# Attention with routed experts on one core: block-wide additions in the last stage, shared-expert work moved ahead of the router's column transposition, and the first query tile projected earlier

## The chip, the cores and the metric

The kernel runs on one NeuronCore of a Trainium2 chip. The time is the device time of a whole run in microseconds (us). Three runs of the kernel before gave 494.02, 495.47 and 496.73 us; the median is 495.47 us.

A core has five engines, each with an instruction stream of its own: TensorE (PE, matrix products into PSUM; PEld is its weight load), VectorE (DVE), ScalarE (ACT), GpSimd (POOL) and SyncE (SP, here used to issue DMAs). DMAs can be issued from SP, ACT or POOL; each engine works through its stream in order, so a DMA that waits for its data holds up what stands behind it on the issuing engine.

## What is computed

All arithmetic is in float32; x has 32 sequences of 100 tokens with 256 features (3,200 tokens), the context 32 sequences of 361 rows with 192 features.

```python
x = x + cross_attention(layernorm(x), ctx)      # one head, E = 256, its own layer norms inside
n = layernorm(x)
shared = gelu(n @ ws1 + bs1) @ ws2 + bs2
aff    = softmax(n @ Wr + br)                   # 31 experts
routed = sum over the 3 best experts e of aff[e] * (gelu(n @ We1[e] + Be1[e]) @ We2[e] + Be2[e])
out    = x + (shared + routed + n)
```

## The kernel before, in words

Tokens lie in 25 tiles of 128, and four tiles make a block (`BLOCKS`: blocks 0 to 5 have four tiles, block 6 has one). `xb[k]` holds block k of the residual stream in SBUF as [128, tiles, 256]. The order on all engines is written out by hand (`manual_schedule`), so program order is execution order on each engine.

**Start.** Wq, Wk, Wv are transposed on TensorE (`transposed`, L300 to L311) and folded into one matrix for the scores (`fold_scores`). Statistics of context rows and tokens are taken on DVE, a rough inverse root on POOL (`rough`, L213, a power), and a Newton step on DVE (`newton`).

**Attention loop, i = 0 to 36** (`for i in range(B + 5)`, B = 32). Every iteration works on several stages at once: the context of sequence i is transposed (`ctx_transpose`, L484), the context of i + 1 normalised (`ctx_normalise`, L474 on ACT and L227 on DVE), the scores of i - 1 taken (`scores`, L492, which needs the projected queries `qk` of its tokens), their exponentials transposed (`exp_transpose`) and applied (`weighted`). `token_project(t)` (L452 on TensorE, L456 on ACT) writes the queries of tile t; for i = 0 that is tile 0, at the end of the iteration's main part. At the end of iteration 0 `transposed(wv_sb, ...)` transposes Wv, and in iteration 1 `bias_cols` (L318) makes Wv's bias columns.

**Router, in the same loop.** Each finished tile passes through `project_out`, `route_norm`, `route_turn` (tile `pl`, L631), `route_logits` (`pr`, L638), `route_choice` (DVE and ACT: the three best experts and a mask `mk`), `route_count` (`pp`, L677 to L681: how many tokens chose each expert so far; POOL adds the running sum, L684), `route_slots` and `route_scatter` (POOL, three indirect DMAs per tile, L559, that write the token's row into its experts' lists in DRAM). Tile 24 is the last: its logits come in iteration 35 (B + 3), its count in 36.

**Shared expert.** `shared_half(k, f, psum)` (L729) is half of a block's first layer, two products of 512 columns; `shared_gelu(k)` (L737) the activation of both halves; `shared_mm(t)` (L752, L755) a tile's second layer together with the gated output biases; `shared_add(t)` (L760) adds it to `xb`. In the loop block 0's halves stand at i = 33 (B + 1) and 35 (B + 3). After the loop come gelu of block 0 and both halves of block 1.

**From counts to experts** (L896 to L990). On DVE: counts are turned into tiles per expert and running ends (a doubling scan, L909, five additions of 31 elements over padded rows `run0`, `run1`), then into a start row and an expert for each of up to 105 expert tiles, two columns `both`. TensorE transposes these columns (`p_ec`, L938); from the result come the numbers with which SP addresses the expert weights and token rows (`fetch`), and the packed expert numbers that TensorE reads as registers. `shared_mm(0)` and `(1)` stand after that transposition, `(2)` ahead of the transposition `p_oh` (L975), `(3)` after it. Then the expert biases are gathered (L984), registers loaded, and block 1's shared second layer is done (`shared_second(1)`).

**Expert stage** (`run`, L1051 to L1084): 92 tiles, each turned, multiplied by its expert's two matrices, scaled and scattered to `y_d` by POOL. A rarely needed rest stands behind an If.

**Last stage** (`TAIL`). Letters and block numbers are the order: f = both halves and gelu of a block, e = its second layer with `shared_add`, t = `total_of`, s = `store`. For each tile `collect` loads the three expert outputs of 128 tokens (384 KB) through SP into one of 15 buffers. `total_of` adds y0 + y1 on POOL (L1147) and x + y2 and x + (y0 + y1) on DVE (L1148, L1149), 256 elements wide, tile by tile. `store` writes a block from ACT's queue (L1154):

```python
TAIL = "f2 f3 e2 t0 t1 f4 s0 s1 e3 t2 t3 f5 s2 s3 e4 t4 f6 s4 e5 t5 s5 e6 t6 s6"
```

Of the kernel before, what the change touches and what calls it, by code (L numbers as in the profile page):

```python
# [8 lines left out]
F32 = mybir.dt.float32  # L9
# [26 lines left out]
def xattn_ffn(  # L36
# [6 lines left out]
    P = 128  # L43
# [43 lines left out]
    def ps_t(name):  # L87
        return ps.tile([P, 512], F32, tag="tp", name=name)
# [303 lines left out]
    pool.memset(ones, 1.0)  # L392

    GM = 4
    PAD = 16
# [7 lines left out]
    for t in XG[0]:  # L403
# [5 lines left out]
    token_rstd(0)  # L409

    kk = iota_t([P, GM, KTOP], "kk", [[0, GM], [1, KTOP]])
    one, oh, onesf, *runs = (
        const.tile([P, n], F32, tag=name, name=name)
        for name, n in (("one", NE), ("oh", NG), ("onesf", P), ("run0", PAD + NE), ("run1", PAD + NE))
    )
    for t_ in (one, onesf):
        pool.memset(t_, 1.0)
    for t_ in (oh, b2z, *runs):
        pool.memset(t_, 0.0)

    mv2 = const.tile([P, NT, 2], F32, tag="mv2", name="mv2")
# [25 lines left out]
    def token_project(t):  # L447
        z = zT.pop(t)
        pq = ps_m(f"pq_{t}")
        for c, s, m in AUG:  # L450
            for d in range(2):
                nc.tensor.matmul(  # L452
                    pq[:m, c * P : (c + 1) * P], m_sb[:, d, s : s + m], z[:, d, :], start=(d == 0), stop=(d == 1)
                )
        for c, s, m in AUG:
            nc.scalar.activation(  # L456
                qk[:m, c, t * P : (t + 1) * P], pq[:m, c * P : (c + 1) * P], AF.Identity,
                bias=c_sb[:m, c : c + 1], scale=vcol[:m, c, G2 : G2 + 1],
            )
# [264 lines left out]
    def shared_half(k, f, psum):  # L724

        n = len(BLOCKS[k]) * P
        ph = phs[k, f] = psum(f"phs_{k}_{f}")
        for c in range(2):
            nc.tensor.matmul(  # L729
                ph[:, :n], ws1_sb[:, c, f::2], xT[k][:, c, :], start=(c == 0), stop=(c == 1)  # L730
            )
# [16 lines left out]
    def shared_mm(t):  # L748
        k, j = divmod(t, TPB)
        h, py = hs[k], ps_t(f"pys_{t}")  # L750
        for f in range(2):
            nc.tensor.matmul(  # L752
                py[:, :D1], h[:, f, j * P : (j + 1) * P], ws2_sb[:, f, :], start=(f == 0), stop=False
            )
        nc.tensor.matmul(py[:, :D1], gT[k], b2z[:, j, :], start=False, stop=True)  # L755
        pys[t] = py

    def shared_add(t):
        xt, _, _ = tile_of(t)
# [14 lines left out]
    def projected(i):  # L774

        return [t for t in range(NT) if t * P // L1 == i]
# [27 lines left out]
    for i in range(B + 5):  # L804
# [35 lines left out]
                route_transpose(t)  # L840
        if i < B:
            ctx_transpose(i)
        if i in crstd:
            ctx_rstd(crstd[i])
        if i + 1 < B:
# [14 lines left out]
            token_norm(t)  # L860
        for t in logits:
            route_logits(t)
        for t in projected(i):
            token_project(t)
        for t in projected(i + 1):
            token_transpose(t)
# [5 lines left out]
            project_out(t)  # L872
        if now:
            route_var(now)
        if i == 0:
            transposed(wv_sb, KD2, wvT, "v")
        if i == 1:
            bias_cols(wv_sb, KD2, B2, BV, lambda ec: wvT[:, ec, D2:DA], "bvc")
        if i == 2:
            fold_values()  # L880
# [2 lines left out]

        if i == B + 1:
            shared_half(0, 0, ps_t)
        if i == B + 3:
            shared_half(0, 1, ps_t)
    residual_factors(slice(EARLY * TPB, NT))
    shared_gelu(0)
    shared_first(1)  # L890

    att_ctx.close()

# [3 lines left out]
    def sel_t(shape, name, dt=F32):  # L897
        return sel.tile(shape, dt, tag=name, name=name)
# [4 lines left out]
    nc.vector.tensor_scalar(nt_i, cnt_i, 7, None, ALU.logical_shift_right)  # L903
    ntf = sel_t([P, NE], "ntf")
    nc.vector.tensor_copy(ntf, nt_i)
    nc.vector.tensor_copy(runs[0][:, PAD:], nt_i)
    cur, step = 0, 1
    while step < NE:
        nc.vector.tensor_tensor(  # L909
            runs[1 - cur][:, PAD:], runs[cur][:, PAD:], runs[cur][:, PAD - step : PAD - step + NE], ALU.add  # L910
        )
        cur, step = 1 - cur, 2 * step
    ends = runs[cur][:, PAD:]
    ind = sel_t([P, NE], "ind")
    ei = sel_t([P, 1], "ei")
    st0 = sel_t([P, 1], "st0")
# [3 lines left out]
    nc.vector.scalar_tensor_tensor(ind, iota0, ei, cnt, ALU.is_equal, ALU.mult, accum_out=nn)  # L920

    j128 = sel_t([P, 1], "j128")
    nc.vector.tensor_tensor(j128, iota_p, st0, ALU.subtract)
    nc.vector.tensor_scalar(j128, j128, float(P), None, ALU.mult)
    start = sel_t([P, 1], "start")
    nc.vector.scalar_tensor_tensor(start, nn, float(-P), j128, ALU.add, ALU.min)
    nc.vector.tensor_scalar(start, start, 0.0, None, ALU.max)
# [20 lines left out]
        nc.vector.scalar_tensor_tensor(ep, e4[:, :, k], float(1 << (BITS * k)), ep, ALU.mult, ALU.add)  # L948
    epT = sel_t([1, P // PACK], "epT", I32)
    nc.vector.tensor_copy(epT, ep)  # L950

    shared_mm(0)
    shared_mm(1)


    diag = sel_t([P, 2 * P], "diag")
# [13 lines left out]


    nc.vector.tensor_scalar(oh[:, :NE], iota0, ec, None, ALU.is_equal)
    shared_mm(2)
    pt = ps_t("p_oh")
    nc.tensor.transpose(pt[:NG, :P], oh, ident)  # L975
    ohT = sel_t([NG, P], "ohT")
    nc.scalar.copy(ohT, pt[:NG, :P])
    for t in range(2):
        shared_add(t)
    shared_mm(3)  # L980
    b1t = const.tile([P, 2, P], F32, tag="b1t", name="b1t")
    for c in range(2):
        pm = ps_m(f"p_b1_{c}")
# [149 lines left out]

    yv = y_d[: KTOP * T, :].rearrange("(t p k) d -> t p (k d)", p=P, k=KTOP)
    slot_ctx.close()
    ypool = ctx.enter_context(tc.tile_pool(name="ypool", bufs=15, reuse_waits="tile"))
    y3s = {}

    def collect(t):
        y3 = y3s[t] = ypool.tile([P, KTOP, D1], F32, tag="y3", name=f"y3_{t}")  # L1140
        reads("y", nc.sync.dma_start(y3.rearrange("p k d -> p (k d)"), yv[t]))

    def total_of(k):
        tiles = BLOCKS[k]
        for j, t in enumerate(tiles):
            y3, xt = y3s.pop(t), xb[k][:, j, :]
            nc.gpsimd.tensor_tensor(y3[:, 0, :], y3[:, 0, :], y3[:, 1, :], ALU.add)  # L1147
            nc.vector.tensor_tensor(xt, xt, y3[:, 2, :], ALU.add)  # L1148
            nc.vector.tensor_tensor(xt, xt, y3[:, 0, :], ALU.add)  # L1149
# [9 lines left out]
    for k in range(3):  # L1159
        for t in BLOCKS[k]:  # L1160
            collect(t)
    TAIL = "f2 f3 e2 t0 t1 f4 s0 s1 e3 t2 t3 f5 s2 s3 e4 t4 f6 s4 e5 t5 s5 e6 t6 s6"
    what = {"f": shared_first, "e": shared_second, "t": total_of, "s": store}
    with tc.manual_schedule(engines={ET.PE, ET.DVE, ET.Activation, ET.Pool}):
        for step in TAIL.split():
            k = int(step[1:])
            what[step[0]](k)
            if step[0] == "t" and k + 3 < len(BLOCKS):
                for t in BLOCKS[k + 3]:
                    collect(t)  # L1170


# [33 lines left out]
```

## Time and profile before

| quantity | value |
|---|---|
| median of three runs | 495.47 us |
| the profiled execution's own time | 495.27 us |
| span of its instructions | 493.5 us |
| mean granted TensorE clock | 0.971 |
| busy: PE, DVE, ACT, POOL | 458.0, 312.3, 248.8, 271.4 us |
| expert stage, about 250 to 440 us | 190 us, PE busy 189.09 |
| last stage, from the first `phs` at 441.56 us | DVE's last addition ends at 490.04 us |
| HBM | 68.27 MB read, 29.74 MB written |

The profile comes from one execution. A row of the timeline gives the start and the length in us, the engine, the line, the operation with its output and inputs, how many instructions were merged, and in brackets how long the engine had stood idle and what released it. Rows of the stretches give the busy time of each engine with its instruction count, then the granted clock of TensorE (1.00 is full speed), the share of time in which the DMA engines were busy and the GB/s they moved. The chain that ended last follows the work back from the last instruction to what released each step.

### The profile page before, as it was taken

How to read it: one execution, taken by the hardware profiler on the slowest of the kernel's cores; microseconds unless marked ns; L12 is line 12 of the kernel's file. 1: busy time of each engine (PE TensorE's matmuls, PEld its weight loads, DVE VectorE, ACT ScalarE, POOL GpSimd, SP SyncE). 2: the span in 40 equal slices, each digit the busy share in tenths (PEclk: the TensorE clock that was granted, in tenths of full speed). 3: DMA queues.
4: the chain of work that ended last, by engine and by line, in shares of the span. 5: the costliest groups of instructions: out<-in, count | busy, mean ns of one | idle time of the engine just before them, and what ended most of it. 6: DMA issues, size and time to landing. Idle time of an engine off the chain costs nothing. (4 is left out here: it accounts for less than half of the span.)

```text
span 493.5 us, 11028 instructions
## 1 busy us (share of the span) xinstructions
PE 458.0 (93%) x2976; PEld 399.5 (81%) x2976; DVE 312.3 (63%) x1280; ACT 248.8 (50%) x814; POOL 271.4 (55%) x544
## 2 busy tenths in 40 slices
PE   8799998998989999997899999999999999989964
PEld 8687877877878888874599999999999999966653
DVE  2789987988998877676554444444444434312995
ACT  2576776776878787745224444444444444432100
POOL 6322686885767575658305555555555555553750
PEclk9799998998999999998999999999999999999977
DMA  6889954453536811212578988888888889426992
GB/s 192 244 223 242 283 144 127 145 164 101 176 99 181 293 58 53 74 42 87 174 237 260 258 261 258 263 260 253 265 271 255 260 270 267 124 79 242 405 322 96
DMA packets 67783, 98.79 MB, mean 200 GB/s; under 512 B 8289, under 2 KB 43176, under 8 KB 67720
## 3 DMA queue, kind: packets, MB, share of 16 engines
q1 hardware_dynamic: 56360, 72.60, 50.8%
q0 software_dynamic: 8048, 22.17, 11.8%
q10 hardware_dynamic: 3312, 3.28, 1.9%
q8 instruction: 28, 0.46, 0.4%
q14 instruction: 35, 0.29, 0.2%
HBM read 68.27 MB, written 29.74 MB: 199 GB/s over the span
## 5 line engine op out<-in xcount | busy, mean ns | idle before, releaser
L559 POOL DMA_INDIRECT y_d<-ys,yrow x92 | 88.3, 960 | 100.3 <-ACT ys L1082 43.4
L1066 ACT ACTIVATE hT<-ph,b1t 128x128 f32<-128x128 f32 x184 | 57.5, 363 | 103.4 <-PE ph L1061 103.4
L1061 PE MATMUL ph<-xgT,w 128*128 128x128 f32 x736 | 101.8, 281 | 0.1
L1061 PEld LDWEIGHTS ph<-xgT,w 128*128 128x128 f32 x736 | 94.8, 197 | 0.4 <-DVE xgT L1053 0.3
L1076 PE MATMUL py<-w2r,hT 128*128 x368 | 94.3, 380 | 0.0
L559 POOL DMA_INDIRECT xs_d<-xl,su x75 | 75.1, 1001 | 28.2 <-issue 8.6
L1076 PEld LDWEIGHTS py<-w2r,hT 128*128 128x128 f32 x368 | 62.9, 190 | 4.8
L1084 DVE TENSOR_SCALAR ys<-py,gate 128x256 f32<-128x256 f32 x46 | 22.2, 484 | 65.4 <-PE py L1076 65.4
L1053 DVE COPY xgT<-pg 128x256 f32<-128x256 f32 x92 | 38.5, 420 | 33.8 <-PE pg L1051 33.8
L492 PE MATMUL pss<-z2T,qk 65*100 65x361 f32 (+1 forms) x128 | 45.7, 479 | 2.4 <-ACT qk L456 2.1
L521 PE MATMUL pcx<-exT,z 128*65 128x100 f32 (+3 forms) x384 | 45.5, 270 | 0.1
L521 PEld LDWEIGHTS pcx<-exT,z 128*65 128x65 f32 (+3 forms) x384 | 41.9, 172 | 0.6 <-ACT exT L508 0.6
L1051 PEld LDWEIGHTS pg<-ident,xg 128*128 128x128 f32 x184 | 35.6, 196 | 4.0
L1051 PE MATMUL pg<-ident,xg 128*128 128x128 f32 x184 | 35.5, 277 | 0.0
L752 PE MATMUL pys<-ws_sb,hs 128*128 128x256 f32 x100 | 27.7, 402 | 5.7 <-DVE x L760 4.6
L242 DVE BATCH_NORM_STATS2 stc<-z 128x6 f32<-128x192 f32 (+1 forms) x96 | 27.8, 344 | 6.9 <-DMA z<-in_ctx_dram 6.9
L1147 POOL TENSOR_TENSOR y<-y 128x256 f32<-128x256 f32 x25 | 20.2, 810 | 18.4 <-PE pys L755 9.2
L537 PE MATMUL po<-wvo,cT 128*128 128x257 f32 (+1 forms) x100 | 26.9, 391 | 3.0 <-ACT cT L528 2.8
L499 ACT ACTIVATE ex<-pss,nm 100x361 f32<-100x361 f32 x32 | 18.0, 562 | 22.3 <-DVE nm L497 19.0
L492 PEld LDWEIGHTS pss<-z2T,qk 65*100 65x100 f32 (+1 forms) x128 | 19.0, 168 | 12.6 <-ACT qk L456 3.5
L752 PEld LDWEIGHTS pys<-ws_sb,hs 128*128 128x128 f32 x100 | 19.8, 202 | 10.7 <-issue 7.8
L452 PE MATMUL pq<-zT,m_sb 128*128 128x128 f32 (+1 forms) x200 | 28.2, 284 | 0.0
(231 smaller groups left out, 868.5 us busy)
## 6 DMA issues: line engine op xcount, KB each, us to landing
w<-in_L_ffn_We_dram SPq DMA_DIRECT2D x92, 256.0 KB
xg<-xs_d SPq DMA_DIRECT2D x92, 131.5 KB
y<-y_d SPq DMA_DIRECT2D x25, 384.0 KB
w2r<-in_L_ffn_We_dram SPq DMA_DIRECT2D x31, 256.0 KB
z<-in_ctx_dram SPq DMA_DIRECT2D x32, 192.0 KB
xs_d<-none SPq DMA_DIRECT2D x3, 1052.0 KB
out_dram<-x ACTq DMA_DIRECT2D x6, 512.0 KB
x<-in_x_dram SPq DMA_DIRECT2D x5, 512.0 KB
```

The costliest lines, as they stand in the source:

```text
L242: nc.vector.bn_stats(st[:n, c, :], ztile[b][:n, c, :D2])
L452: nc.tensor.matmul(pq[:m, c * P : (c + 1) * P], m_sb[:, d, s : s + m], z[:, d, :], start=(d == 0), stop=(d == 1))
L492: nc.tensor.matmul(pss[:L1, :L2], qk[:m, a, b * L1 : (b + 1) * L1], z2T[:m, a, :], start=(a == 0), stop=(a == 1),)
L521: nc.tensor.matmul(pw[:m, :L1], z[:n, c, s : s + m], exT[:n, c, :], start=(c == 0), stop=(c == NCH - 1))
L537: nc.tensor.matmul(po[:, : D1 + 1], cT[:m, a, t * P % RING : t * P % RING + P], wvo[:m, a, :], start=(a == 0), stop=(a == 1))
L559: ins = nc.gpsimd.indirect_dma_start(out=dst, out_offset=bass.IndirectOffsetOnAxis(ap=index, axis=0), in_=src, in_offset=None).ins
L752: nc.tensor.matmul(py[:, :D1], h[:, f, j * P : (j + 1) * P], ws2_sb[:, f, :], start=(f == 0), stop=False)
L1051: nc.tensor.transpose(pt[:, c * P : (c + 1) * P], g[:, c::2], ident)
L1053: nc.vector.tensor_copy(xgT[i].rearrange("p c s -> p (c s)"), pt[:, : 2 * P])
L1061: nc.tensor.matmul(ph[:, f * P : (f + 1) * P], w1s[:, c, f::2], z[:, c, :], start=(c == 0), stop=(c == 1))
L1066: nc.scalar.activation(hT[i][:, f, :], ph[:, f * P : (f + 1) * P], AF.Gelu, bias=b1t[:, f, i : i + 1])
L1076: nc.tensor.matmul(py[:, :D1], h[:, f, :], w2f[:, bass.ds(e * (2 * D1) + f * D1, D1)], start=(f == 0), stop=(f == 1),)
```

## The change

- Last stage: `collect` loads a whole block into one buffer of [128, 4, 3, 256], still with one DMA a tile; five such buffers take the place of 15 tile buffers. `total_of` does all three additions on DVE, for blocks 0 to 4 over the whole block (1,024 elements a partition), for block 5 in two pairs of tiles (512), for block 6 over its one tile. The shared second layer is done in pairs: two tiles' products go into the two halves of one PSUM bank (`two_second`), and one addition of 512 takes them. Stores of blocks 0 to 4 are issued from POOL, those of 5 and 6 from ACT. The order in `TAIL` is new.
- Router's end: half (0, 1) moves from i = B + 3 to i = B + 2, half (1, 0) takes its place, and half (1, 1), tiles 0 and 1 of block 0 and block 1's gelu follow directly behind the loop, ahead of `p_ec`. Tiles 2 and 3 stand between `p_ec` and `p_bc`. `pys_3` takes its bank from the other PSUM ring.
- On DVE the doubling scan becomes one scan instruction, and j128 one instruction instead of two; the padded rows and their two memsets go.
- Start: tile 0 is projected in the middle of iteration 0, behind the transposition of context 0 and ahead of the normalisation of context 1; the transposition of Wv moves from iteration 0 to iteration 1.

```diff
@@ attention loop @@
         if i < B:
             ctx_transpose(i)
+        if i == 0:
+            for t in projected(i):
+                token_project(t)
...
-        for t in projected(i):
+        for t in projected(i) if i else ():
             token_project(t)
...
-        if i == 0:
+        if i == 1:
             transposed(wv_sb, KD2, wvT, "v")
-        if i == 1:
             bias_cols(wv_sb, KD2, B2, BV, lambda ec: wvT[:, ec, D2:DA], "bvc")
...
         if i == B + 1:
             shared_half(0, 0, ps_t)
+        if i == B + 2:
+            shared_half(0, 1, ps_t)
         if i == B + 3:
-            shared_half(0, 1, ps_t)
+            shared_half(1, 0, ps_m)
     residual_factors(slice(EARLY * TPB, NT))
     shared_gelu(0)
-    shared_first(1)
+    shared_half(1, 1, ps_m)
+    for t in range(2):
+        shared_mm(t)
+    shared_gelu(1)
@@ from counts to experts @@
-    nc.vector.tensor_copy(runs[0][:, PAD:], nt_i)
-    cur, step = 0, 1
-    while step < NE:
-        nc.vector.tensor_tensor(
-            runs[1 - cur][:, PAD:], runs[cur][:, PAD:], runs[cur][:, PAD - step : PAD - step + NE], ALU.add
-        )
-        cur, step = 1 - cur, 2 * step
-    ends = runs[cur][:, PAD:]
+    ends = sel_t([P, NE], "ends")
+    nc.vector.tensor_tensor_scan(ends, one, ntf, 0.0, ALU.mult, ALU.add)
...
-    nc.vector.tensor_tensor(j128, iota_p, st0, ALU.subtract)
-    nc.vector.tensor_scalar(j128, j128, float(P), None, ALU.mult)
+    nc.vector.tensor_scalar(j128, iota_p, st0, float(P), ALU.subtract, ALU.mult)
...
-    shared_mm(0)
-    shared_mm(1)
+    shared_mm(2)
+    pys[3] = ps_m("pys_3")
+    shared_mm(3, pys[3])
...
-    shared_mm(2)
     pt = ps_t("p_oh")
...
-    shared_mm(3)
@@ last stage @@
-    ypool = ctx.enter_context(tc.tile_pool(name="ypool", bufs=15, reuse_waits="tile"))
+    ypool = ctx.enter_context(tc.tile_pool(name="ypool", bufs=5, reuse_waits="tile"))
...
+    def collect(k):
+        y3 = y3s[k] = ypool.tile([P, TPB, KTOP, D1], F32, tag="y3", name=f"y3_{k}")
+        for j, t in enumerate(BLOCKS[k]):
+            reads("y", nc.sync.dma_start(y3[:, j, :, :].rearrange("p k d -> p (k d)"), yv[t]))
 
     def total_of(k):
-        tiles = BLOCKS[k]
-        for j, t in enumerate(tiles):
-            y3, xt = y3s.pop(t), xb[k][:, j, :]
-            nc.gpsimd.tensor_tensor(y3[:, 0, :], y3[:, 0, :], y3[:, 1, :], ALU.add)
-            nc.vector.tensor_tensor(xt, xt, y3[:, 2, :], ALU.add)
-            nc.vector.tensor_tensor(xt, xt, y3[:, 0, :], ALU.add)
+        y3 = y3s.pop(k)
+        n, width = len(BLOCKS[k]), TPB if k < len(BLOCKS) - 2 else TPB // 2
+        for j in range(0, n, width):
+            js = slice(j, min(j + width, n))
+            xt = xb[k][:, js, :]
+            nc.vector.tensor_tensor(y3[:, js, 0, :], y3[:, js, 0, :], y3[:, js, 1, :], ALU.add)
+            nc.vector.tensor_tensor(xt, xt, y3[:, js, 2, :], ALU.add)
+            nc.vector.tensor_tensor(xt, xt, y3[:, js, 0, :], ALU.add)
+
+    def two_second(k):
+        tiles = BLOCKS[k]
+        for j in range(0, len(tiles), 2):
+            pair = tiles[j : j + 2]
+            py = ps_t(f"pyt_{pair[0]}")
+            for i, t in enumerate(pair):
+                shared_mm(t, py[:, i * D1 : (i + 1) * D1])
+            xt = xb[k][:, j : j + len(pair), :].rearrange("p t d -> p (t d)")
+            nc.vector.tensor_tensor(xt, py[:, : len(pair) * D1], xt, ALU.add)
...
-        nc.scalar.dma_start(
+        eng = pool if k < len(BLOCKS) - 2 else nc.scalar
+        eng.dma_start(
...
-    TAIL = "f2 f3 e2 t0 t1 f4 s0 s1 e3 t2 t3 f5 s2 s3 e4 t4 f6 s4 e5 t5 s5 e6 t6 s6"
-    what = {"f": shared_first, "e": shared_second, "t": total_of, "s": store}
+    TAIL = "f2 f3 e2 t0 s0 f4 t1 s1 e3 t2 s2 f5 t3 s3 e4 f6 t4 s4 t5 e5 s5 e6 t6 s6"
+    what = {"f": shared_first, "e": two_second, "t": total_of, "s": store}
```

More of the change, by code (lines that the diff above doesn't have):

```diff
@@ L394, in xattn_ffn @@
     GM = 4
-    PAD = 16
     iota0 = iota_t([P, NE], "iota0", [[1, NE]])
@@ L411, in xattn_ffn @@
     kk = iota_t([P, GM, KTOP], "kk", [[0, GM], [1, KTOP]])
-    one, oh, onesf, *runs = (
-        const.tile([P, n], F32, tag=name, name=name)
-        for name, n in (("one", NE), ("oh", NG), ("onesf", P), ("run0", PAD + NE), ("run1", PAD + NE))
+    one, oh, onesf = (
+        const.tile([P, n], F32, tag=name, name=name) for name, n in (("one", NE), ("oh", NG), ("onesf", P))
     )
@@ L417, in xattn_ffn @@
         pool.memset(t_, 1.0)
-    for t_ in (oh, b2z, *runs):
+    for t_ in (oh, b2z):
         pool.memset(t_, 0.0)
@@ L746, in xattn_ffn, with shared_mm @@
     pys = {}
-    def shared_mm(t):
+    def shared_mm(t, py=None):
         k, j = divmod(t, TPB)
-        h, py = hs[k], ps_t(f"pys_{t}")
+        h = hs[k]
+        if py is None:
+            py = pys[t] = ps_t(f"pys_{t}")
         for f in range(2):
@@ L755, in shared_mm @@
         nc.tensor.matmul(py[:, :D1], gT[k], b2z[:, j, :], start=False, stop=True)
-        pys[t] = py
     def shared_add(t):
@@ L1135, in xattn_ffn @@
     slot_ctx.close()
-    ypool = ctx.enter_context(tc.tile_pool(name="ypool", bufs=15, reuse_waits="tile"))
+    ypool = ctx.enter_context(tc.tile_pool(name="ypool", bufs=5, reuse_waits="tile"))
     y3s = {}
-    def collect(t):
-        y3 = y3s[t] = ypool.tile([P, KTOP, D1], F32, tag="y3", name=f"y3_{t}")
-        reads("y", nc.sync.dma_start(y3.rearrange("p k d -> p (k d)"), yv[t]))
+    def collect(k):
+        y3 = y3s[k] = ypool.tile([P, TPB, KTOP, D1], F32, tag="y3", name=f"y3_{k}")
+        for j, t in enumerate(BLOCKS[k]):
+            reads("y", nc.sync.dma_start(y3[:, j, :, :].rearrange("p k d -> p (k d)"), yv[t]))
     def total_of(k):
-        tiles = BLOCKS[k]
-        for j, t in enumerate(tiles):
-            y3, xt = y3s.pop(t), xb[k][:, j, :]
-            nc.gpsimd.tensor_tensor(y3[:, 0, :], y3[:, 0, :], y3[:, 1, :], ALU.add)
-            nc.vector.tensor_tensor(xt, xt, y3[:, 2, :], ALU.add)
-            nc.vector.tensor_tensor(xt, xt, y3[:, 0, :], ALU.add)
+        y3 = y3s.pop(k)
[7 more added lines that the diff above has]
+    def two_second(k):
+        tiles = BLOCKS[k]
+        for j in range(0, len(tiles), 2):
[5 more added lines that the diff above has]
+            nc.vector.tensor_tensor(xt, py[:, : len(pair) * D1], xt, ALU.add)
     def store(k):
@@ L1153, in store @@
         n = len(tiles) * P
-        nc.scalar.dma_start(
+        eng = pool if k < len(BLOCKS) - 2 else nc.scalar
+        eng.dma_start(
             of[tiles[0] * P : tiles[0] * P + n, :].rearrange("(t p) d -> p t d", p=P), xb[k]
         )
-    for k in range(3):
-        for t in BLOCKS[k]:
-            collect(t)
-    TAIL = "f2 f3 e2 t0 t1 f4 s0 s1 e3 t2 t3 f5 s2 s3 e4 t4 f6 s4 e5 t5 s5 e6 t6 s6"
-    what = {"f": shared_first, "e": shared_second, "t": total_of, "s": store}
+    for k in range(5):
+        collect(k)
+    TAIL = "f2 f3 e2 t0 s0 f4 t1 s1 e3 t2 s2 f5 t3 s3 e4 f6 t4 s4 t5 e5 s5 e6 t6 s6"
+    what = {"f": shared_first, "e": two_second, "t": total_of, "s": store}
     with tc.manual_schedule(engines={ET.PE, ET.DVE, ET.Activation, ET.Pool}):
@@ L1167, in xattn_ffn @@
             what[step[0]](k)
-            if step[0] == "t" and k + 3 < len(BLOCKS):
-                for t in BLOCKS[k + 3]:
-                    collect(t)
+            if step[0] == "t" and k + 5 < len(BLOCKS):
+                collect(k + 5)
 _INS = [
```

## The prediction

> **What bounds the kernel now.** I read the busy time by stretches first, because the whole span mixes stages with different limits.
>
> ```profile
> core 0: us, PE busy (x) PEld busy (x) DVE busy (x) ACT busy (x) POOL busy (x), PEclk, DMA share, GB/s
> 224.00:250.00 26.00, 20.62 (x87) 13.91 (x87) 13.95 (x70) 8.57 (x26) 13.12 (x27) 0.93 0.47 151
> 250.00:440.00 190.00, 189.09 (x1296) 179.44 (x1294) 83.83 (x318) 79.30 (x230) 97.03 (x181) 1.00 0.81 243
> 460.00:475.00 15.00, 12.25 (x52) 8.98 (x50) 13.85 (x27) 1.26 (x2) 9.68 (x12) 1.00 1.04 386
> 475.00:493.50 18.50, 9.21 (x30) 7.37 (x30) 12.66 (x30) 0.62 (x2) 3.38 (x4) 0.69 0.45 157
> ```
>
> The expert stage (250 to 440) is TensorE's, busy 189.09 of 190 us, and the diff does not touch it. What can move are the start, the passage from router to experts (224 to 250) and the last stage (from 441.5). There the chain that ended last runs on DVE's two additions almost without a break from 454 to 476, then through TensorE (its granted clock at half from 476.9 to 481.7) and DVE again. The timeline shows why those additions are slow:
>
> ```profile
> 455.97 1.82 POOL L1147 TENSOR_TENSOR y<-y 128x256 f32<-128x256 f32 x2 [0.25 <-DMA y<-y_d]
> 456.45 0.77 DVE L1149 TENSOR_TENSOR x<-x,y 128x256 f32<-128x256 f32 x1
> ...
> 466.54 1.26 ACT L737 ACTIVATE hs<-phs,b1c 128x512 f32<-128x512 f32 x2 [8.53 <-DVE x L760]
> ...
> 472.70 0.43 DVE L1149 TENSOR_TENSOR x<-x,y 128x256 f32<-128x256 f32 x1
> ...
> 489.62 0.42 DVE L1149 TENSOR_TENSOR x<-x,y 128x256 f32<-128x256 f32 x1
> ```
>
> Beside a POOL addition L1149 takes 0.77 us; at 472.7, with POOL idle and DMA still at 371 GB/s, it takes 0.43. The cause is POOL, not memory traffic. ScalarE's gelu of block 5 waits 8.5 us, because the stores s0 and s1 stand ahead of it on ACT's queue and wait for DVE; that in turn starves TensorE.
>
> **Last stage.** Removed: POOL's 25 additions and 50 narrow DVE additions. Added: three DVE additions per block. From 0.18 us at 31 elements to 0.415 at 256 is 1.04 ns an element, so 512 wide cost 0.68 and 1024 wide 1.21 us (an estimate from those rows; no 1024-wide DVE row exists). Bounds: 4 x 0.34 = 1.36, the closest start-to-start of narrow ones, and 4 x 0.77 = 3.1, if the slow rate stayed. I take 1.21, since the slope is the same over all DVE rows; a faster one has no row.
>
> A full block is 3 x 1.21 = 3.65 us; shared additions become two of 0.68 per block instead of four of 0.42. DVE's work: five blocks 18.2, block 5 in pairs 6 x 0.68 = 4.1, block 6 3 x 0.43 = 1.3, shared 8 x 0.68 + 0.42 = 5.9: 29.5 us, against 35.3 DVE-busy now (16.0 + 12.8 + 6.5).
>
> When can it run? On the old clock: block 2's second shared pair leaves TensorE at 453.9, so t0 starts at 454.6. The y loads move the same bytes at the same rate: 1.98 MB had arrived by 454, then 0.407 MB/us. A tile is 0.393 MB, a store 0.524. With the stores in between, block 1 is complete at 456.9, block 2 at 462, block 3 at 467.2, block 4 at 472.4, block 5 at 477.5. DVE: t0 to 458.2, t1 461.9, e3 463.3, t2 467.0, t3 467.2 to 470.9, e4 (TensorE ready at 471.0) 472.3, t4 476.1, t5 480.2, e5 481.6, e6 482.0, t6 483.3. So DVE and DMA are late together, each within a microsecond of the other. After the last addition now (490.04) the span lasts 3.46 us more for the last store; kept, the end is 486.85 against 493.5: **-6.65**. TensorE (f2 f3 e2 f4 e3 f5 e4 f6 e5 e6, without ACT's block) ends near 478.5 and hides. The ring of y buffers grows from 15 tiles to five blocks, 20 tiles, so loads are requested no later than now: block 5 after t0, block 6 after t1. A DVE chain this full has no cover left: any delay of DVE lands on the end.
>
> Five stores go from ACT's queue to POOL's, where nothing else is queued any more. One costs between 0.73 us (POOL's one direct DMA, 2.01) and four times the 0.96 of a 128-row scatter, 3.8; I take 1. Even 3.8 for s4, issued at 476.1, ends under t5 to t6. Against this speaks the Trainium skill, SBUF — State Buffer, section "SBUF: two separate sides": a DMA from the POOL queue needs descriptors written through a port that DVE in a two-port mode locks. The row nearest:
>
> ```profile
> 234.90 0.98 POOL L559 DMA_INDIRECT xs_d<-xl,su  x1 [0.28 <-POOL xl L699]
> 235.00 1.09 DVE L909 TENSOR_TENSOR run<-run 128x31 f32<-128x31 f32 x5
> ```
>
> Five DVE additions with two inputs in SBUF ran beside a POOL descriptor job, and neither was longer than elsewhere (0.96 to 1.0; 0.19). By the rule, read on DVE in general, five stores would pile up behind t6: 2.62 MB at 0.407 = 6.4 us, and the tail would gain nothing. By the row, 0. I go by the row.
>
> **Passage from router to experts.**
>
> ```profile
> 229.34 3.66 PE L729 MATMUL phs<-qk,ws_sb 128*128 128x512 f32 x4
> ...
> 237.96 0.38 PE L938 MATMUL p_ec<-ident,both 128*1 128x128 f32 x2 [1.02 <-DVE both L931]
> ...
> 246.24 1.10 PE L752 MATMUL pys<-ws_sb,hs 128*128 128x256 f32 x4 [1.07 <-issue]
> ...
> 251.49 0.86 PE L1051 MATMUL pg<-ident,xg 128*128 128x128 f32 x6
> ```
>
> TensorE idles 5.4 of 26 us here, then has shared work to do before the first expert tile at 251.49. The half at 229.34 ran at half clock (1.88 us at full, at 221.86) after a stretch with 1.4 us of matmul in 4; it held the last count back: cnt came at 233.90, though its mask was ready at 230.88.
>
> Now half (0,1) fills 225.43 to 227.3. Behind it on PE wait pl_24 (ready 226.9, so +0.4) and pp_23, whose mask comes only at 228.1: nothing lost. With TensorE kept busy, half (1,0) runs at full clock, 229.3 to 231.1; pp_24 follows; cnt at 232.2 (-1.7). On DVE the scan replaces a cast and five additions: 234.80 to 236.13, 1.33 us, against about 0.25 (nearest: 0.20 for 32 elements); with the fused j128 (0.18), -1.25. `both` is ready at 235.05. But half (1,1) and tiles 0 and 1 (2 x 1.29) now stand ahead of p_ec on PE: they wait for gelu's end at 233.9 (as now) and finish at 236.2. So p_ec moves from 237.96 to 236.2 and the old wait turns into a queue of 1.15 us. Then tiles 2 and 3 to 238.8, p_bc when its diagonal is ready (239.0), p_oh at 240.9 (it now waits for the buffer of pys_0, so for a DVE addition, 0.45), bias columns, two transposes, registers (1.1): shared work of block 1 starts near 243.8 instead of 246.24, and the first expert tile near 249.0: **-2.45**.
>
> What could be late next: SP's third weight load waits for the last scatter, whose issue ends at 238.43, POOL-bound and unmoved; so xg goes out at about 242.1 instead of 242.64 and its first tiles land by 246, three us ahead of need.
>
> A rule weighs on this: TensorE: Matmul & The Clock Gate, Part 1: the clock is halved unless recent activity holds it up, over a window of some 3.4 us, with a phase that varies. The rows: full at 221.86, half at 229.34. If half (0,1) at 225.43 ran at half rate, it would end at 229.1, delay pl_24 and pp_23 by about 2, and cnt would come at 234.3: -0.95 in all instead of -2.45. I take full: less than 2 us lie between matmul stretches there.
>
> **Start.**
>
> ```profile
> 19.27 0.55 ACT L474 ACTIVATE z<-z,cb_c,cr_c 105x192 f32<-105x192 f32 x1 [2.54 <-DVE cb_c L259]
> ...
> 20.21 0.79 ACT L456 ACTIVATE qk<-pq,c_sb,vcol 128x128 f32<-128x128 f32 x2
> ...
> 20.70 2.32 PE L492 MATMUL pss<-z2T,qk 128*100 128x361 f32 x4 [1.77 <-ACT qk L456]
> ```
>
> The queries of tile 0 now go ahead of that ACT wait, so pss starts near 17.6, not 20.70. But the next iteration depends on DVE's factors for sequence 2, which come from POOL's power at 23.52 as before, and the queries of tile 1 leave ACT at about 26.1 instead of 26.5. So most of the 3 us drains away; TensorE, continuous from 24 to 40, keeps about **-0.5** (bounds: -1.5, if PE's idle time goes wholly; +0.3, if DVE's stretch 24 to 33, without a gap, decides). The value transposes of Wv moved to i = 1 cost the same 0.97 and 0.53 us; their bias columns read Wv and not the transposes, so no wait is added. The two dropped POOL memsets (0.21) were beside other work.
>
> Sum on the profiled execution: span 493.5 - 6.65 - 2.45 - 0.5 = 483.9; 1.77 us lie around the span (495.27), so 485.7. The median of the runs is 0.20 higher than the profiled one: **485.9**.
>
> **Rivals.** (a) The passage gives little and the start nothing (half clock, -0.95) and the tail as computed: 495.47 - 7.6 = 487.9. (b) POOL's stores lag behind DVE, or hold the loads up: the tail gains 0 to 4 instead of 6.65, so 488.5 to 492.5, say 490. For it the rule, against it the 0.98 row. (c) Slower: the wide additions don't run at 1.04 ns an element but at the rate seen beside POOL, because the loads write SBUF meanwhile; 15 wide ones at 3.1 instead of 1.21 add 28 us on DVE's full chain: about 514. It turns the result from 1.21 + 9.6/18 = 1.74 us per wide addition on (the 9.6 gained over 18 wide equivalents). Against it: 0.43 at 472.7 under 371 GB/s. (d) The change doesn't do what it says, because y loads and not DVE set the end: if the last tile still lands at 479.5, t6 and a store after it give 479.5 + 1.3 + 3.5 = 484.3 on the old clock, earlier than my 486.85; so loads alone can't undo the gain unless they get slower.
>
> **Chances.** As computed 0.62 (range 484 to 487.5); (a) 0.17; (b) 0.14; (c) and other losses 0.04; about no change 0.03. I leave (c) and the far end of (b) out: 483.2 to 489.3. Under 0.5% (2.5 us, about what a measurement of this kernel tells from no change): faster 0.93, same 0.03, slower 0.04.
>
> **What would show it.** Right: wide additions at 1.2 us, ACT's gelu of block 5 without its 8.5 us wait, granted clock near 1 until the last matmul, cnt about 1.7 us earlier, p_ec behind tile 1 and not behind DVE, first expert tile 2.4 us earlier, pss near 17.6. Wrong: wide additions over 1.4 us, DVE waiting for y loads by more than 2 us, POOL's DMAs ending after t6, a 3.66 us half ahead of pl_24.

## The result, and the profile after

| | before | after |
|---|---|---|
| median of 20 executions, same chip | 496.19 us (492.35 to 499.07) | 492.34 us (484.91 to 494.16) |
| ratio, with its interval | 1 | 0.9874 [0.9843, 0.9906] |
| profiled execution | 495.27 us, span 493.5 | 493.44 us, span 491.7 |
| granted clock of the profiled execution | 0.971 | 0.962 |

The change makes the kernel faster, but by less than forecast: 485.9 of 495.47 is a ratio of 0.9807. The ratio leaves out executions over 1.5% above the fastest of their kernel (for after 11 of the 20, because one took only 484.91 us; for before none), while the median counts all 20. So the gain is 6.3 us (4.7 to 7.8) by the ratio and 3.9 by the medians, where 9.6 were forecast. The profiled execution of after is one of the longer ones.

First the busy time of after by stretches, laid where the stages now lie:

```profile
core 0: us, PE busy (x) PEld busy (x) DVE busy (x) ACT busy (x) POOL busy (x), PEclk, DMA share, GB/s
226.00:254.00 28.00, 23.10 (x94) 15.78 (x93) 15.46 (x74) 9.25 (x31) 15.45 (x31) 0.94 0.43 132
254.00:444.00 190.00, 189.57 (x1298) 179.84 (x1296) 84.14 (x318) 79.08 (x230) 96.61 (x180) 1.00 0.81 245
464.00:479.00 15.00, 15.00 (x67) 11.88 (x66) 14.35 (x15) 2.11 (x4) 3.13 (x4) 1.00 1.03 408
479.00:491.70 12.70, 5.29 (x25) 4.32 (x23) 8.73 (x14) 0.00 (x0) 0.75 (x1) 0.85 0.55 205
```

In the last stage VectorE is still busy almost without a break (14.35 of 15 us), but now in 15 instructions instead of 27. TensorE keeps its full clock until its last product ends at 484.3; before it had half of it from 476.9 to 481.7. The timeline of after shows what the prediction had computed:

```profile
460.30 1.22 DVE L1147 TENSOR_TENSOR y<-y 128x1024 f32<-128x1024 f32 x1
...
464.21 0.84 POOL L1166 DMA_DIRECT2D out_dram<-x  x1 [17.95 <-DVE x L1149]
464.96 1.22 DVE L1148 TENSOR_TENSOR x<-x,y 128x1024 f32<-128x1024 f32 x1
...
470.08 0.69 ACT L735 ACTIVATE hs<-phs,b1c 128x512 f32<-128x512 f32 x1 [6.27 <-PE phs L727]
...
483.81 0.69 DVE L1147 TENSOR_TENSOR y<-y 128x512 f32<-128x512 f32 x1 [0.62 <-DMA y<-y_d]
```

A 1024-wide addition takes 1.22 us (estimated 1.21), the store on POOL's queue 0.84, the gelu of block 5 waits for its own matmul and not for stores, and the loads hold VectorE up for 0.62 us in all. The chain that ended last, though, runs in this profile along the loads of y and not along VectorE's additions:

```profile
471.39 12.40 DMA y<-y_d
```

Loads and VectorE end together, as computed, so little is left to gain from VectorE alone. The passage is another matter. TensorE there:

```profile
241.00 0.38 PE L937 MATMUL p_ec<-ident,both 128*1 128x128 f32 x2
...
243.86 0.67 PE L961 MATMUL p_bc<-diag,onesf 128*128 128x256 f32 x2
245.40 0.27 PE L973 MATMUL p_oh<-ident,oh 128*32 128x128 f32 x1 [0.87 <-DVE oh L971]
246.01 0.73 PE L981 MATMUL p_b<-ohT,b1r 32*128 32x128 f32 x4 [0.34 <-ACT ohT L975]
246.68 0.44 PE L713 MATMUL pg<-ident,gates 128*128 128x128 f32 x2
249.04 2.05 PE L752 MATMUL pys<-ws_sb,hs 128*128 128x256 f32 x4 [1.92 <-issue]
...
255.96 0.87 PE L1048 MATMUL pg<-ident,xg 128*128 128x128 f32 x6
```

From 244 to 249 TensorE has 2.1 us of work, then stands 1.92 us at its register loads ("issue" in the row; 1.07 before), and comes back at half clock: the first products of block 1 take 2.05 us where before they took 1.10.

Three starts and the end cut the span into stages: half (0,0), the first expert tile, the last stage's phs. "Front" is all that lies ahead of half (0,0), "passage" what lies between it and the first expert tile.

| us in one profile | front, to half (0,0) | passage | experts | last stage |
|---|---|---|---|---|
| before | 221.86 | 29.63 | 190.07 | 51.94 |
| after | 226.65 | 29.31 | 189.70 | 46.04 |
| predicted difference | -0.5 | -2.45 | 0 | -6.65 |
| measured difference | +4.79 | -0.32 | -0.37 | -5.90 |

So the experiments have to say whether the front's 4.79 us belongs to the change, and why the passage gave nothing. **Theory A**: the front is nearly the same loop in both kernels, and its loss comes from how long TensorE happens to stand at half clock in one execution. **Rival B**: the new start causes it. **Theory C**: the passage's gain is real but is lost at the register loads and to the half clock behind them. **Rival D**: something else sets the first expert tile.

### The profile page after: what moved, and what is told of

Read it like the earlier page. It is cut to its first block, busy times and chain, and to the rows that moved or that the text cites. A ratio compares the mean times of both kernels' runs of the same rounds, so it can differ in the third digit from the quotient of the medians.

```text
span 491.7 us, 10908 instructions
## 1 busy us (share of the span) xinstructions
PE 462.9 (94%) x2976; PEld 403.6 (82%) x2976; DVE 306.4 (62%) x1240; ACT 248.9 (51%) x814; POOL 254.5 (52%) x522
## 4 chain that ended last, share of the span: by engine, by line
PE 52%; DVE 24%; DMA 8%; POOL 7%; issue 5%; ACT 3%; SPq 1%; POOLq 0%; DVEq 0%; ACTq 0%
PE ph L1058 16%; PE py L1073 15%; DMA y<-y_d 6%; PE pg L1048 4%; POOL xs_d L557 3%; DVE stc L242 3%; PE pcx L519 2%; PE pq L450 2%; DVE x L540 2%; PE pss L490 2%; DVE z L227 2%; PE pys L752 2%; DVE st_m L201 2%; DVE nm L495 2%; DMA y_d<-ys,yrow 2%
## 5 line engine op out<-in xcount | busy, mean ns | idle before, releaser
L450 PE MATMUL pq<-zT,m_sb 128*128 128x128 f32 (+1 forms) x200 | 30.5, 300 | 0.0
L482 PE MATMUL pz<-ident,z 128*128 128x128 f32 (+2 forms) x192 | 27.9, 283 | 0.0
L1079 ACT ACTIVATE ys<-py,gate 128x256 f32<-128x256 f32 x46 | 21.8, 474 | 11.5 <-ACT hT L1063 9.7
L727 PE MATMUL phs<-qk,ws_sb 128*128 128x512 f32 (+1 forms) x56 | 24.9, 587 | 2.0 <-PEq L1125 2.0
```

The lines of the kernel that those rows point to most:

```text
L450: nc.tensor.matmul(pq[:m, c * P : (c + 1) * P], m_sb[:, d, s : s + m], z[:, d, :], start=(d == 0), stop=(d == 1))
```

## The experiments

| kernel | its median, us | before on its chip | ratio [interval] | front | passage | last stage |
|---|---|---|---|---|---|---|
| e_tail | 492.3 | 499.79 | 0.9854 [0.9813, 0.9895] | 226.69 | 30.33 | 45.13 |
| e_pass | 500.1 | 499.79 | 1.0007 [0.9986, 1.0029] | 222.73 | 30.05 | 51.73 |
| e_start | 499.15 | 499.79 | 0.9976 [0.9954, 0.9997] | 225.19 | 30.33 | 53.38 |
| e_nostart | 491.99 | 499.79 | 0.9843 [0.9802, 0.9884] | 224.07 | 30.93 | 45.77 |
| e_again | 489.84 | 495.49 | 0.985 [0.9803, 0.9897] | 224.68 | 29.36 | 45.17 |
| e_spread | 486.7 | 495.49 | 0.9826 [0.9791, 0.9862] | 223.66 | 25.67 | 46.13 |
| e_regs | 486.23 | 495.49 | 0.9819 [0.9774, 0.9863] | 225.54 | 25.48 | 45.46 |
| e_gates | 487.81 | 495.49 | 0.9851 [0.9822, 0.9881] | 220.56 | 30.30 | 45.23 |
| e_best | 483.3 | 495.26 | 0.976 [0.9737, 0.9783] | 216.19 | 27.16 | 45.28 |
| e_bregs | 494.88 | 495.26 | 0.9997 [0.9974, 1.002] | 223.48 | 28.93 | 53.45 |
| e_actstore | 491.72 | 495.26 | 0.9888 [0.9841, 0.9936] | 222.82 | 29.24 | 45.81 |
| e_pooladd | 494.16 | 495.26 | 0.9915 [0.9879, 0.9951] | 223.75 | 30.31 | 48.19 |
| e_fill | 493.53 | 500.01 | 0.9864 [0.9823, 0.9904] | 228.98 | 32.34 | 45.4 |
| e_bgates | 495.82 | 500.01 | 0.9913 [0.988, 0.9946] | 224.67 | 30.01 | 52.11 |
| e_best_ns | 490.15 | 500.01 | 0.9774 [0.972, 0.9829] | 221.51 | 30.83 | 45.28 |

The stage columns are from one profile each, the ratios from repeated executions. A profile is one draw: those of e_pass and e_best took the least time of all executions of their kernel, those of e_fill and e_bgates the most. Kernels with the same "before" time ran on the same chip.

**The parts alone: e_tail, e_pass, e_start, e_nostart.** Each is the kernel before with some hunks of the change's own diff.

```diff
 e_tail     the last stage's hunks (collect, total_of, two_second, store, TAIL)
 e_pass     the passage's hunks (halves, shared_mm order, scan, j128)
 e_start    the start's hunks (token_project(0), transposed(wv_sb))
 e_nostart  e_tail and e_pass together
```

> The kernel before with the new last stage alone (wide additions on VectorE, shared halves in pairs, stores of blocks 0 to 4 on GpSimd's queue). The prediction gave this part -6.65 us; the trace of the full change shows -5.90 from the first phs to the end of the span, of which 1.7 went to phs at half clock. Both theories (the loop lost to the granted clock by chance; the loop lost to the new start) leave this part alone: -5.5 to -6.7 us against before, ratio 0.9865 to 0.989. If only -4 or less comes, the last stage itself gives less than its own trace shows.

> The kernel before with the new passage from router to experts alone (shared halves and tiles 0 and 1 ahead of the numbers, scan, fused j128). Predicted -2.45 us. Theory A (half-clock stretches in the passage took the gain back, as the trace of the full change shows with block 1's first shared product at 2.05 instead of 1.03 us): -0.3 to -2.0 by the phase of the clock, -1.2 in the median. Rival B (the new start costs): the passage keeps its -2.45. From half (0,0) to the first expert tile before took 29.63 us; A expects 27.6 to 29.3 here, B 27.2.

> The kernel before with the new start alone (queries of tile 0 ahead of the wait for the columns of sequence 0, transposition of Wv in iteration 1). Predicted -0.5 us. Rival B (the new start moves the later work so that TensorE loses its clock more often in the attention loop): +3 to +5 us, half (0,0) near 225 to 227 instead of 221.86. Theory A (the loop's loss in the profiled run was a matter of the clock's phase in that run): within 1 us of before, half (0,0) anywhere from 220 to 227.

> The full change with its start undone: new passage and new last stage only. Prediction's terms: 493.5 - 6.65 - 2.45, so -9.1 us against before. Rival B: 3 to 5 us below the full change, so -7 to -9 against before. Theory A: as the full change within 1.5 us, so -3 to -6 against before.

Measured: the last stage alone 0.9854 of 499.79, -7.3 us (-9.3 to -5.3), against -6.65 computed. The passage alone +0.3 us (-0.7 to +1.4), against -2.45, and in its profile it is no shorter (30.05; 29.63 to 30.33 in the four profiles of the old order). The start alone -1.2 us (-2.3 to -0.1), against -0.5. Passage and last stage together -7.8 us (-9.9 to -5.8): more than theory A had said (-3 to -6), which had gone by the full change's medians, and within what rival B had said (-7 to -9). But B needed +3 to +5 for the start alone, and so it falls. The front agrees. Up to half (0,0) e_tail is the kernel before, instruction for instruction; its profile there reads

```profile
226.69 1.88 PE L729 MATMUL phs<-qk,ws_sb 128*128 128x512 f32 x4
```

which is 4.83 us later than in the profile of before, and as late as in after. The chip is not the reason: e_pass and e_nostart, with the same front on the same chip, reached half (0,0) at 222.73 and 224.07. The five profiles with the old front (before, e_tail, e_pass, e_nostart, e_bregs) span 221.86 to 226.69, and the prediction's base was the lowest of them. What differs is the clock. Added up over stretches of 1 us, TensorE stood at half clock for 13.6 us of before's front, 20.5 of e_tail's and 27.3 of after's, and was busy for 206.28, 209.87 and 212.24 us with the same products.

A smaller cost of the new start is not excluded. The eight profiles that have it with the old loop average 225.2 at half (0,0), the five old fronts 223.8; the timing of e_start points the other way.

**Where the front loses: e_again, e_gates, e_bgates.** Rows of after's TensorE in the loop:

```profile
113.66 0.45 PE L713 MATMUL pg<-ident,gates 128*128 128x128 f32 x1 [2.19 <-DVE gates L668]
...
115.10 2.48 PE L519 MATMUL pcx<-exT,z 128*128 128x100 f32 x12
...
124.08 1.35 PE L519 MATMUL pcx<-exT,z 128*128 128x100 f32 x12
```

TensorE waits 2.19 us for the gates of a block, then runs without a gap, but at half clock (2.48 for a product that takes 1.35 nine us later). The wait is in before too (2.18); how long the half clock lasts differs. By the granted clock of 2-us stretches it lasted 3.4 us in before (0.83, 0.50, 0.82 from 112 to 118) and 10.2 us in after (0.62, four times 0.50, 0.82 from 112 to 124).

```diff
         for t in slots:
...
             route_scatter(t)
-            if i <= B:
-                route_transpose(t)
...
             project_out(t)
+        for t in slots:
+            if i <= B:
+                route_transpose(t)
```

> The full change once more, on the chip of the next three, as their mark. From its parts: last stage -7.3, passage +0.3, start -1.2 us, so -8 against before, ratio 0.984. By theory A (clock's phase in the attention loop differs from run to run) half (0,0) lies anywhere from 221 to 227 us although the loop is the same; by rival B (start costs) again at 226 to 227. From half (0,0) to the first expert tile 29.3 to 31, block 1's first shared product at half clock (2.05 us).

> The full change with the transpositions of gates in the attention loop moved to the end of their iteration, so that TensorE does not wait for VectorE there (1.43, 2.19 and 1.71 us in the trace, and half-clock stretches of up to 10 us behind them). Theory A: the three waits and the half-clock stretches behind them go; half (0,0) at 217 to 221 instead of 221 to 227, 3 to 6 us faster than the full change, and a narrower spread over the runs. Rival E (VectorE bounds the loop there, and TensorE's clock doesn't matter): within 1 us of the full change, the wait turns up at another TensorE line of the same iteration.

> The kernel before with only the gates' transpositions in the attention loop moved to the end of their iteration. Theory A (TensorE's waits of 1.4 to 2.2 us in the loop and the half-clock stretches behind them cost time in every version): -2 to -4 us against before, half (0,0) at 217 to 221 us. Rival (the loop's time is VectorE's, the move helped only by chance): within 1 us of before.

The full change again gave 0.985, with a front of 224.68. With the gates' transpositions at the end of their iteration the front fell to 220.56 in the profile and the median by 2.0 us against e_again, but the ratio is the same (0.9851). Theory A had expected 3 to 6 us. On the full change the gain of the move alone is not shown; part of the wait comes back at another line, as rival E had said:

```profile
114.74 0.68 PE L636 MATMUL pr<-wr,qk 128*128 128x31 f32 x4 [1.37 <-ACT qk L630]
...
146.37 0.63 PE L636 MATMUL pr<-wr,qk 128*128 128x31 f32 x4 [1.06 <-ACT qk L630]
```

The same move in the kernel before gave 0.9913 [0.988, 0.9946], -4.4 us: there it pays, though where the time is gained no profile shows. The one there is missed the expected front (224.67, not 217 to 221); it is of the longest of seven executions.

**Where the passage loses: e_regs, e_spread, e_bregs.**

```diff
 # e_regs: on the full change; e_bregs: the same on the kernel before
-    total = registers()
     shared_second(1)
+    total = registers()
 # e_spread: as e_regs, and tile 3 behind p_bc instead of ahead of it
-    pys[3] = ps_m("pys_3")
-    shared_mm(3, pys[3])
...
     nc.vector.tensor_scalar(oh[:, :NE], iota0, ec, None, ALU.is_equal)
+    pys[3] = ps_m("pys_3")
+    shared_mm(3, pys[3])
```

> The full change with one line moved: block 1's second half ahead of TensorE's register loads. It shows which half of theory C counts: the wait on the registers (then hidden from the clock behind full work, -1 to -2 us against the full change), or the thin stretch before it (then the first product of block 1 still runs at half clock and the gain is 0 to -1).

> The full change with TensorE's shared work spread over the passage: tile 3 between the two broadcasts' steps again, and block 1's second half ahead of the register loads instead of behind them. Theory C (the passage gave nothing, since all shared work went ahead of the numbers, TensorE then idled from 244 to 249 and came back at half clock): block 1's first product takes 1.03 us, not 2.05, and from half (0,0) to the first expert tile 27 to 28 us instead of 29.3 to 31; 2 to 3 us faster than the full change. Rival D (the loads of registers or SyncE's fetches set the first expert tile, whatever TensorE does): unchanged within 0.5 us, with the wait in front of the first expert tile.

> The kernel before with only block 1's second half moved ahead of TensorE's register loads. Theory C (the new order of the passage was worth its -2.45 us or more and the register wait with the half clock behind it ate it): here TensorE stood only 1.07 us at the loads and came back at full clock, so this move alone gives -1.0 to -1.3 us, and from half (0,0) to the first expert tile 28.3 to 29.3 us against 25.5 with the new order. Rival F (the move is the whole gain, and the new order of the passage is worth nothing): -3.5 us, and some 26 us.

One moved line took 3.9 us out of the passage (29.36 in e_again, 25.48 in e_regs). The median fell by 3.6 us, the ratio by 1.5 us, and the intervals overlap, so this pair's timing settles nothing. Another pair does: e_best, below, is e_gates with this one line moved, and their intervals do not meet (0.9851 [0.9822, 0.9881] and 0.976 [0.9737, 0.9783], 4.5 us). e_regs' TensorE:

```profile
245.56 0.44 PE L713 MATMUL pg<-ident,gates 128*128 128x128 f32 x2
245.84 1.03 PE L752 MATMUL pys<-ws_sb,hs 128*128 128x256 f32 x4
...
250.59 0.59 PE L755 MATMUL pys<-b2z,gT 128*128 128x256 f32 x2
251.02 0.94 PE L1048 MATMUL pg<-ident,xg 128*128 128x128 f32 x6
```

No wait is left in front of the first expert tile, so rival D falls, and block 1 runs at full clock. The loads cost 1.92 us where TensorE had nothing queued; behind 5.2 us of queued products they cost nothing. The likely reason is the queue, which is 64 deep by the Trainium skill (TensorE: Matmul & The Clock Gate, the table ahead of its first section): 24 products with as many weight loads stand ahead here, and the register loads can pass while the array works them off. No run varies the number queued. e_spread, which also fills the thin stretch, adds nothing (25.67). In the kernel before the same move shortens the passage to 28.93 and the time not measurably (expected -1.0 to -1.3; the interval reaches from -1.3 to +1.0). So rival F falls, which had this move alone worth 3.5 us. In favour of theory C, the new order with the loads out of the way takes 25.48 us in e_regs and 25.67 in e_spread, against 28.93 in the old one. But the two later kernels with that order took 27.16 (e_best) and 30.83 (e_best_ns), so the 3.4 us between 28.93 and 25.48 are what the order can give, not what it always gives.

**Wait or clock: e_fill, e_best.**

```diff
 # e_fill: on the full change
+    filler = ps_t("filler")
+    for _ in range(9):
+        nc.tensor.matmul(filler[:, :P], ident, ident, start=True, stop=True)
     total = registers()
     shared_second(1)
 # e_best: the full change with the edits of e_regs and e_gates
```

> The full change with nine throwaway products (128x128, 0.22 us each, some 1.95 us together, their result is never read) on TensorE between the last gates' transposition and its register loads; nothing else moves. Theory C1 (the half clock behind the wait is the larger part): the products fill the wait, block 1's first product starts no earlier but runs at 1.03 us, not 2.05, and from half (0,0) to the first expert tile takes 26.5 to 27.8 us instead of 29.3; 1.5 to 2.5 us faster than the full change although it computes more. Rival C2 (the register loads themselves take TensorE's time, one after the other, and the clock is a side issue): the products add to the loads, 29.5 to 31.3 us, 0 to 2 us slower than the full change.

> The full change with both repairs: block 1's second half ahead of TensorE's register loads (worth -3.6 us in its own run) and the gates' transpositions at the end of their iteration (-2.0). Added up -5.6 against the full change, so some 484.3 where before takes 495.5, ratio 0.977. If the two gains have the same root in the clock (a stretch at half clock less in front moves the next one), they don't add: -3.6 to -4.5.

e_fill decided nothing: 0.9864 is near the full change's own ratios, and its passage of 32.34 us lies outside both expectations. Its rows show why:

```profile
251.57 4.05 PE L1123 MATMUL filler<-ident 128*128 128x128 f32 x18
255.41 1.76 PE L752 MATMUL pys<-ws_sb,hs 128*128 128x256 f32 x4
```

The throwaway products (nine, in 18 passes) ran at half clock themselves, 4.05 us instead of 1.95: in this profile the clock was lost ahead of them. VectorE was late as well (p_bc waited 1.53 us for it), and p_b took 1.18 us where after's took 0.73. The rows above answer better. After's wait is 1.92 us, and its block 1, from the first product to the first expert tile, takes 6.92 us (249.04 to 255.96) against 5.18 in e_regs (245.84 to 251.02). So wait and half clock are about equal parts, 1.9 and 1.7. e_best shows that the half clock can come without the wait: in its profile block 1's first two tiles fell on it (1.25 + 1.06 + 1.91 + 0.84 us of products for 1.03 + 0.59 + 1.03 + 0.59), and its passage took 27.16 us, 1.7 more than e_regs'. As the two edits' sum had it (0.977), e_best gave 0.976 [0.9737, 0.9783], -11.9 us: faster than both kernels, 483.3 us in its median. The page of its profiled execution, the shortest of six (480.3 us), shows a loop without a half-clock slice:

```profile
span 478.5 us, 10902 instructions
...
PEclk9999999999999999999999999999999999999997
```

**The start, priced again: e_best_ns.** e_best with the start's hunks undone.

```diff
-        if i == 0:
-            for t in projected(i):
-                token_project(t)
...
-        for t in projected(i) if i else ():
+        for t in projected(i):
```

> The best version so far (full change, block 1's second half ahead of the register loads, gates' transpositions at the end of their iteration) with the new start undone. It prices the start where the loop behind it is steadier. Prediction's term: the start is worth -0.5, so +0.5 us against the best version (ratio to before 0.977 instead of 0.976). Rival B: the new start costs 3 to 5 us, so this one is faster by that (0.967 to 0.970). A result within 1 us either way says that the start carries nothing through the loop.

0.9774 [0.972, 0.9829] against 0.976 with the start: 0.7 us, of the size expected and within the uncertainty. The 3 to 5 us that rival B expected this kernel to gain (0.967 to 0.970) lie outside the interval.

**The last stage's cause: e_actstore, e_pooladd.**

```diff
 # e_actstore: on the full change
-        eng = pool if k < len(BLOCKS) - 2 else nc.scalar
-        eng.dma_start(
+        nc.scalar.dma_start(
 # e_pooladd: e_actstore, and
-            nc.vector.tensor_tensor(y3[:, js, 0, :], y3[:, js, 0, :], y3[:, js, 1, :], ALU.add)
+            nc.gpsimd.tensor_tensor(y3[:, js, 0, :], y3[:, js, 0, :], y3[:, js, 1, :], ALU.add)
```

> The full change with the stores of blocks 0 to 4 back on ScalarE's queue. It prices the move to GpSimd's queue. The prediction priced a store there at 1 us beside other work: the trace shows 0.75 to 0.84 us, no lag. ScalarE's gelu of blocks 4 and 5 then wait for stores again (about 2.7 us), ahead of products that are not needed for 5 us: 0 to +1 us against the full change. If descriptors written by GpSimd had held VectorE or the loads up, this one is faster by 1 to 4 us.

> As the run with the stores on ScalarE, and with the first of the three wide additions (y0+y1) on GpSimd again, all of them 1024 wide. It tests the cause named for the last stage, GpSimd's additions slowing VectorE's: wide additions on VectorE then take 1.22 us where GpSimd rests and 1.9 to 2.4 beside it (0.77 to 0.42 in the kernel before), GpSimd's own about 3.2 (4 x 0.81), and the last stage is 1 to 4 us longer than with all three on VectorE. If width alone made the gain, VectorE keeps 1.22 and with a third less work ends no later: 0 to -1.

With the stores back on ScalarE the last stage is as long (45.81 against 45.13 to 46.13 in the others): in these profiles the queue of the stores is worth nothing either way. With POOL's addition back it is 48.19, outside that range and 2.4 us longer than e_actstore's. The time agrees but doesn't prove it: 2.4 us by the medians, 1.3 by the ratios, whose intervals overlap.

```profile
460.63 3.11 POOL L1147 TENSOR_TENSOR y<-y 128x1024 f32<-128x1024 f32 x1 [0.36 <-DMA y<-y_d]
461.45 3.38 DVE L1148 TENSOR_TENSOR x<-x,y 128x1024 f32<-128x1024 f32 x1
...
469.24 1.21 DVE L1148 TENSOR_TENSOR x<-x,y 128x1024 f32<-128x1024 f32 x1
469.59 3.06 POOL L1147 TENSOR_TENSOR y<-y 128x1024 f32<-128x1024 f32 x1 [2.56 <-DVE x L1160]
```

The same wide addition takes 3.38 us where it starts 0.82 us behind POOL's, and 1.21 where it starts 0.35 us ahead of it. The slow one shares 2.29 us with POOL's (461.45 to 463.74) and is 2.17 us longer: it stands nearly still while POOL adds. This is what the Trainium skill has for two such operations (SBUF — State Buffer, "Who interferes with whom": an exclusive lock).

One of the three additions was taken off VectorE, and the stage grew longer; so POOL's additions do slow VectorE down, as predicted. They are not the whole gain. With POOL adding again the stage of 48.19 us is still 4.3 shorter than the 52.5 that the old form takes on average. That larger part belongs to the rest of the new last stage (fewer and wider additions, paired shared tiles, the order, the larger buffers), which no run takes apart. "Not the width" is not shown.

## Why the prediction was right, and where it was wrong

**Last stage, -6.65: right.** Alone -7.3 us; over the profiles its length is 52.5 us on average in the old form (five) and 45.5 in the new one (eleven with VectorE adding). The prices held: 1.22 and 0.69 us for the wide additions, 0.75 to 0.84 for a store on POOL (1 assumed), 3.2 us behind the last addition (3.46). (The sum's own figures, 483.3 + 3.46, give 486.76 and so -6.74; the slip of 0.09 us changes nothing.) VectorE and the loads ended within 0.62 us of each other, as computed. Of the cause, POOL's 2.4 us are shown and the other 4.3 are not divided. The Trainium skill's rule (SBUF — State Buffer, "SBUF: two separate sides") speaks of a two-port mode of VectorE; the prediction read it on VectorE in general, and that reading fails here: five stores went out from POOL beside wide additions in 0.75 to 0.84 us each. Rival (c), 3.1 us for a wide addition, is about what e_pooladd shows beside POOL (2.12 to 3.38); with no addition on POOL it does not happen, even at 408 GB/s.

**Passage, -2.45: the step that failed.** Up to p_ec all came as computed: cnt 1.69 us earlier against half (0,0) (forecast 1.7), p_ec 1.75 earlier (1.76), behind tile 1 and not behind VectorE. The failed step reads "bias columns, two transposes, registers (1.1): shared work of block 1 starts near 243.8 instead of 246.24, and the first expert tile near 249.0". Two terms of it were mis-sized. The 1.1 for the registers was taken from the old order, in which tile 2 stood right ahead of p_oh and tile 3 behind it, so that TensorE had work queued; the change moved both ahead, and the wait measured 1.92. And block 1 was given its 5.25 us of before; at half clock it took 6.92. On before's scale block 1 began at 244.25 (forecast 243.8) and the first expert tile at 251.17 (forecast 249.0, 251.49 before). The seven other profiles with the new order and the loads ahead show this passage at 29.2 to 32.3 us, and timing puts it at +0.3 us. The clock's rule had been weighed at half (0,1), where full clock was right (1.97 us), and not some 18 us later, where this change makes the hole. Rival (a) had half clock in the passage, but at the wrong place and with half of the size. That its 487.9 lies nearer to the measured times is partly luck.

**Start, -0.5: not contradicted, hardly shown.** -1.2 us alone (-2.3 to -0.1) and 0.7 in the pair e_best and e_best_ns; but e_nostart, without it, was no slower than the full change (0.9843 against 0.9874 and 0.985). Its mark failed:

```profile
15.38 1.41 PE L482 MATMUL pz<-ident,z 128*128 128x128 f32 x6
16.58 1.95 PE L450 MATMUL pq<-zT,m_sb 128*128 128x128 f32 x8
19.08 2.05 PE L490 MATMUL pss<-z2T,qk 128*100 128x361 f32 x4
```

pss came at 19.08, not 17.6, because the context's transposition and the queries of tile 0 behind it ran at half clock (before they took 0.79 and 1.15 us).

**The part left alone was not constant.** The sum stood on one profile, whose front of 221.86 us was the shortest of five with the same code; that was luck of the draw. In after's profile 4.79 us went there, with 27.3 us at half clock for 13.6, and none of it is shown to be the change's.

The sum by the measured parts is -7.3 + 0.3 - 1.2 = -8.2 us of 499.79, a ratio of 0.9836. That is inside the interval of e_again and just below that of the first measurement (0.9843 to 0.9906). Between the forecast 0.9807 and 0.9874 lie 3.3 us; the passage's 2.8 (from -2.45 to +0.3) are most of it. The median of 492.34 is 2.4 us above 0.9874 of before's 496.19; the executions spread with the clock (484.91 at a granted clock of 0.983, 493.4 at 0.962), and e_again's median was 489.84 of 495.49. Whether the full change is worth nearer 4 or nearer 7 us stays open.

## What to carry to other kernels

Work pulled forward past a serial chain leaves a hole where it was; look at what that work had been covering, register loads and the matmul clock included, before counting the gain. Where registers are loaded on TensorE, put the loads behind queued matmuls, not ahead of them. A sum on one profile inherits the luck of the stages that the change does not touch, so take their spread from several profiles. And when an experiment puts the supposed cause back, compare how much of the gain it takes away: here it was 2.4 of 7.0 us.

## What the runs showed of the hardware beyond that

- A wait of about 2 us does not always halve the clock, and the half clock does not always last equally long. The last stage's phs, behind a gap of 1.8 to 2.4 us in all kernels, took 7.11 us in ten profiles (before, e_pass, e_best among them) and 8.81 in seven (after, e_again, e_regs among them). In the loop the half clock lasted 3.4 us in before and 10.2 us in after, though TensorE had work again after 2.2 us. Over a whole front it adds up to multiples of 3.4 us: 6.8 us in e_best_ns, 13.6 in before, 20.5 in e_tail, 27.3 in after. The Trainium skill (TensorE: Matmul & The Clock Gate, Part 1) has the clock return after at least one busy window of some 3.4 us, with a phase that varies; the multiples agree, and why it took three windows in after no run shows.
- In three profiles (e_nostart, e_fill, e_best_ns) VectorE took up p_ec 1.4 to 2.3 us later than in the nine others of that order, and the trace shows nothing that held it (in e_nostart it stood idle for 1.5 us after p_ec had ended). The cause is open.
